# Layer 3 of a four-layer graph kernel: values and sums of weights in separate 32-column tiles, shares made before the transposes, some sums added on VectorE, and a new order of the work

## The chip, the cores and the metric

The kernel runs on one core of one Trainium2 chip. The metric is the time of one execution on the device in microseconds; the time of a kernel is the median over its runs. The engines named below are TensorE (PE in the profile), VectorE (DVE), ScalarE (ACT), GpSimd (POOL) and SyncE (SP). Each engine works through its own instructions strictly in the order in which the program lists them, and they meet at semaphores.

## What is computed

There are 16 graphs of 1024 nodes with 128 features, and a 0/1 adjacency matrix for each. Four layers follow each other, and each adds its result to its input and normalises the sum over the features (`x = layernorm(x + layer(x, adj))`). Layers 0 and 1 are graph attention (1 head of 128 features; 8 heads of 16), layer 2 is an average over neighbours with learned matrices. Layer 3, which the change is about, is dot-product attention with 4 heads of 32 features over the neighbours:

```python
Wh = jnp.einsum('bsf,hfd->bhsd', features, W)                    # 4 heads, D = 32
scores = jnp.einsum('bhsd,bhtd->bhst', Wh, Wh) / jnp.sqrt(jnp.float32(D))
scores = jnp.where(adj_matrix[:, None, :, :] > 0, scores, NEG_INF)
attn = jax.nn.softmax(scores, axis=-1)
h = jnp.einsum('bhst,bhtd->bhsd', attn, Wh)
```

The softmax is never made as such. The kernel makes the weights exp(score), sums weight times value and weight alone over the neighbours on TensorE, and divides the first sum by the second at the end.

## The kernel before

**Who decides the order.** The kernel does not write its instructions in the order in which they run. Each piece of work is a `step` with an engine, a planned duration, a due time (`due`) and the buffers that it reads and writes. `Plan.run` replays these steps against planned clocks: of all steps whose inputs are ready, it takes for each engine the one that can start first, and among those that could start within 0.05 us of each other the one with the earliest due time. A step is not considered before its due time is within `AHEAD` of the earliest open one. The order that comes out is written into the program and is fixed; on the chip every engine keeps to it, whatever the real durations are. Due times are offsets in a graph's own time, which advances by `PERIOD` from graph to graph, so that layer 3 of one graph is mixed with layers 0, 1 and 2 of the next ones. Planned durations are numbers in the source (`step("DVE", 1.07, at, share, ...)`).

**Buffers.** Steps claim places in pools. In PSUM there are two places `wk` of two banks each, used for scores, products and transposes, two places `acc1` of one bank (sums of layers 0 and 1) and two places `acc3` of one bank (sums of layer 3). In SBUF the pool `z` (9 places) holds the weights of layers 0 and 1, and `z3` (4 places) those of layer 3.

**Layer 1** is the largest load of VectorE: for each of 8 blocks of 128 nodes and each of 8 heads, `scalar_tensor_tensor` over 128x1024 makes the weights `z` (line 774). TensorE multiplies them with the values (line 782), with four heads side by side in 32 columns each.

**Layer 3** is the nested loop in `layer3`: two halves of 512 columns, and in each half 8 blocks `j` of 128 nodes. For a block, ScalarE makes `gap` (line 1060, very large where there is no edge), TensorE makes four heads of scores in two `wk` places (lines 1070 and 1080, in row tiles), ScalarE takes their exponential into two `z3` places of two heads each (line 1113), and `weighted` multiplies them with the values (line 1092). The values of a head carry a column of ones, so a head has 33 columns and takes a 64-column tile; one call of `weighted` covers two heads, and a block needs two calls. The two accumulators `av` hold values and sum of weights together.

At the end of a half ScalarE copies both accumulators to `oT` (line 1129), TensorE transposes 8 blocks (line 362), and VectorE takes the reciprocals of the sums, one per node and head (`share`, lines 1140 and 1143), multiplies, and adds the result to `x3` (line 1154).

**Around it.** `before3` prepares layer 3: a transposed input, the product with the weights in a `wk` place, a copy `whT`, seven small copies that turn the heads by groups of 32 rows (`turn`, lines 1004 and 1006, read from the same `wk` place), a transpose of those, the values `hh3`, and a bound on the scores from squared norms (lines 1030 and 1037). Each layer ends in `layernorm`: VectorE makes `off` (line 420), ScalarE squares eight blocks (line 426), VectorE makes the variance (line 437), GpSimd takes its power -1/2 (line 442), VectorE makes `shift` (line 448), ScalarE applies both (line 454). Layer 2's goes on with gamma, beta, relu and a sum on VectorE (lines 951, 958, 965) and a second normalisation.

Of the kernel before, what the change touches and what calls it, by code (L numbers as in the profile page):

```python
# [20 lines left out]
F32 = mybir.dt.float32  # L21
BF16 = mybir.dt.bfloat16
I32 = mybir.dt.int32
AF = mybir.ActivationFunctionType
# [52 lines left out]
class Plan:  # L77
# [6 lines left out]
    SLACK = 0.00  # L84
    SWITCH = 0.1
    SAME = 0.0
    AHEAD = 327.0

    def __init__(self):
        self.steps = []  # L90
        self.places = {}
        self.users = {}
        self.turns = {}

# [8 lines left out]
    def step(self, engine, us, due, emit, reads=(), writes=(), lag=None, holds=(), floor=0.0, mode="full"):  # L103
# [28 lines left out]
        follows.discard(s)  # L132
        s.waits = len(follows)
# [87 lines left out]
def tile_binary(  # L221
# [32 lines left out]
    W3 = D3 + 1  # L254
    F8 = mybir.dt.float8e5
    PAD1 = 32 - W1
    PAD3 = 64 - W3
# [10 lines left out]
    make_identity(nc, ident)  # L268
    far = const.tile([P, P], BF16, name="far")
# [17 lines left out]
    LATER1 = 3.4  # L287
    LATER3 = 13.7
# [27 lines left out]

    plan.pool("wk", wks)
# [5 lines left out]
    places("z3", 4, [P, 2, HALF])  # L323
    places("oT1", 1, [P, N])
    places("oT3", 1, [P, N])
# [17 lines left out]
    for t in places("hh3", 3, [P, HB, H3 * W3 + PAD3]):  # L343
        nc.vector.memset(t[:, :, : H3 * W3].rearrange("p k (h c) -> p k h c", c=W3)[:, :, :, D3:], 1.0)
        nc.vector.memset(t[:, :, H3 * W3 :], 0.0)
# [629 lines left out]
    def before3(b, due):  # L975
# [7 lines left out]
        def heads(hh):  # L983
            return hh.t[:, :, : H3 * W3].rearrange("p k (h c) -> p k h c", c=W3)[:, :, :, :D3]

        for chunk in range(2):
# [5 lines left out]
                [xT, w3c], [(ps, 0)], holds=[hh, whT, turn],  # L992
# [3 lines left out]
                [(ps, 0)], [whT],  # L996
            )

            def turned_groups(turn=turn, ps=ps):
                for h in range(H3):  # L1000
                    rows_h = slice(h * D3, (h + 1) * D3)
                    into = blocks_of(turn.t[rows_h, :])
                    of = blocks_of(ps.t[rows_h, :HALF])
                    nc.scalar.copy(into[:, :, h * D3 :], of[:, :, : P - h * D3])  # L1004
                    if h:
                        nc.scalar.copy(into[:, :, : h * D3], of[:, :, P - h * D3 :])

            step("ACT", 2.6, due + chunk, turned_groups, [(ps, 0)], [turn])
            step(
                "PE", 0.44, due + chunk,  # L1010
                lambda turn=turn, ps=ps: transposes(
                    ps.t[:, HALF:], [turn.t[:, k * P : (k + 1) * P] for k in range(HB)]
                ),
                [turn], [(ps, 1)],
# [3 lines left out]
                lambda hh=hh, ps=ps: nc.scalar.copy(  # L1018
                    heads(hh), ps.t[:, HALF:].rearrange("p (k h d) -> p k h d", k=HB, h=H3)
                ),  # L1020
                [(ps, 1)], [hh],
# [3 lines left out]
        sq, norms, bound = Buf("oT3", "sq"), little("norms", [P, NB * H3]), little("bound", [P, 1])  # L1025
        low = G["low"] = little("low", [P, 1])
        for n, hh in enumerate(hhs):
            step(
                "ACT", 0.48, due,
                lambda n=n, hh=hh: nc.scalar.activation(  # L1030
                    sq.t.rearrange("p (c k h d) -> p c k h d", c=2, k=HB, h=H3)[:, n], heads(hh), AF.Square
                ),
                [hh], [(sq, n)],
            )

        def largest():
            nc.vector.tensor_reduce(norms.t, sq.t.rearrange("p (n d) -> p n d", d=D3), AX.X, ALU.add)
            nc.vector.tensor_reduce(bound.t, norms.t, AX.X, ALU.max)

        step("DVE", 1.35, due, largest, [sq], [norms, bound])  # L1040
# [8 lines left out]
    def layer3(b, due, span):  # L1049
        G = graphs[b]  # L1050
        x3, m, whTs, turns, low, hhs = G["x3"], G["m"], G["whT"], G["turn"], G["low"], G["hh3"]
        tot = little("tot", [P, NB])
        for half in range(2):
            cols = slice(half * HALF, (half + 1) * HALF)
            av = [Buf("acc3", f"av3_{g}") for g in range(2)]
# [33 lines left out]
            def weighted(j, g, z, av=av):  # L1089
# [80 lines left out]

    PERIOD = 133.3
    weights(-190)
    for b in range(B):
        at = b * PERIOD
# [637 lines left out]
```

## Time and profile before

| | |
|---|---|
| median of 3 runs | 2353.89 us (2352.1 to 2354.01) |
| profiled execution | 2357.02 us, span of its instructions 2355.2 us |
| PE, PE weight loads | 2144.1 us (91%), 996.5 us (42%) |
| DVE, ACT, POOL | 1875.7 us (80%), 1707.9 us (73%), 286.7 us (12%) |
| mean granted TensorE clock | 0.976 |

Busy time is the union of an engine's instructions. A matmul in float32 stands in the trace as two instructions, and four column tiles run side by side, so the mean length of one matmul says little; the distance from the start of one group to the start of the next is what TensorE really spends. From about 459 us to 2145 us one stretch of 135.04 us repeats, one for each graph; before it the pipeline of graphs fills, and after 2145 us only layers 2 and 3 of the last graphs are left.

### The profile page before, as it was taken

How to read it: one execution, taken by the hardware profiler on the slowest of the kernel's cores; microseconds unless marked ns; L12 is line 12 of the kernel's file. 1: busy time of each engine (PE TensorE's matmuls, PEld its weight loads, DVE VectorE, ACT ScalarE, POOL GpSimd, SP SyncE). 2: the span in 40 equal slices, each digit the busy share in tenths (PEclk: the TensorE clock that was granted, in tenths of full speed). 3: DMA queues.
4: the chain of work that ended last, by engine and by line, in shares of the span. 5: the costliest groups of instructions: out<-in, count | busy, mean ns of one | idle time of the engine just before them, and what ended most of it. 6: DMA issues, size and time to landing. Idle time of an engine off the chain costs nothing.

```text
span 2355.2 us, 47149 instructions
## 1 busy us (share of the span) xinstructions
PE 2144.1 (91%) x19376; PEld 996.5 (42%) x19376; DVE 1875.7 (80%) x2616; ACT 1707.9 (73%) x4214; POOL 286.7 (12%) x268
## 2 busy tenths in 40 slices
PE   5758899999999999999999999999999999998776
PEld 5515354443625445352534444363544436242321
DVE  4899888979797988979797897979789797995201
ACT  3414669698786969788686869868686987869675
POOL 2001011111011111111011111101111110110000
PEclk8879999999999999999999999999999999999988
DMA  6222221313122221312232131313213031200000
GB/s 103 57 65 32 82 37 52 72 24 87 32 82 37 83 40 24 87 41 78 33 95 31 33 92 24 84 26 97 32 57 66 14 87 24 73 10 10 1 10 11
DMA packets 80817, 119.32 MB, mean 51 GB/s; under 512 B 7384, under 2 KB 58704, under 8 KB 80592
## 3 DMA queue, kind: packets, MB, share of 16 engines
q1 hardware_dynamic: 62160, 99.43, 13.1%
q0 software_dynamic: 18432, 16.79, 8.7%
q8 instruction: 154, 2.52, 0.4%
q14 instruction: 71, 0.58, 0.1%
HBM read 157.55 MB, written 8.97 MB: 71 GB/s over the span
## 4 chain that ended last, share of the span: by engine, by line
PE 52%; DVE 24%; ACT 19%; issue 2%; POOL 1%; DMA 1%; POOLq 0%; DVEq 0%; ACTq 0%
PE acc L1092 15%; DVE z L774 13%; PE acc L782 10%; PE wk L1080 7%; PE acc L634 7%; ACT z L1113 5%; ACT junk L426 4%; PE wk L371 4%; PE wk L362 3%; ACT x L454 3%; PE wk L1070 2%; ACT turn L1004 2%; PE wk L914 2%; DVE tot L401 2%; DVE x L935 1%
## 5 line engine op out<-in xcount | busy, mean ns | idle before, releaser
L774 DVE SCALAR_TENSOR_TENSOR z<-R,q,m 128x1024 f32<-128x1024 f32 x1024 | 1249.8, 1278 | 53.2 <-PE acc L782 45.4
L1092 PE MATMUL acc<-z,hh 128*64 128x512 f32 x2048 | 546.9, 621 | 70.8 <-ACT z L1113 70.8
L1113 ACT ACTIVATE z<-wk,low 128x1024 f32<-128x1024 f32 x512 | 542.6, 1105 | 74.4 <-PE wk L1080 74.4
L782 PE MATMUL acc<-z,hh 128*32 128x512 f32 x4096 | 517.3, 615 | 60.6 <-DVE z L774 58.0
L426 ACT ACTIVATE junk<-x,off 128x128 f32<-128x128 f32 x640 | 257.3, 402 | 302.6 <-DVE off L420 286.0
L442 POOL TENSOR_TENSOR rstd<-rstd,b_neg_half 128x8 f32<-128x8 f32 (+1 forms) x81 | 176.1, 2174 | 1308.1 <-DVE rstd L437 1192.2
L1080 PE MATMUL wk<-whT,turn 32*128 32x512 f32 x2048 | 295.8, 647 | 0.0
L454 ACT ACTIVATE x<-x,shift,rstd 128x128 f32<-128x128 f32 x640 | 256.5, 488 | 31.7 <-DVE shift L448 31.7
L1092 PEld LDWEIGHTS acc<-z,hh 128*64 128x64 f32 x2048 | 106.4, 136 | 393.8 <-ACT z L1113 196.0
L634 PEld LDWEIGHTS acc<-hd,z 128*128 128x128 f32 x2048 | 243.6, 195 | 67.0 <-issue 18.5
L782 PEld LDWEIGHTS acc<-z,hh 128*32 128x32 f32 x4096 | 103.6, 110 | 389.5 <-issue 205.9
L634 PE MATMUL acc<-hd,z 128*128 128x129 f32 x2048 | 259.9, 282 | 7.0 <-DVE z L622 3.8
L914 PEld LDWEIGHTS <-m 128*128 128x128 fp8e5 x3072 | 178.6, 98 | 16.9 <-issue 16.8
L914 PE MATMUL wk<-y,m 128*128 128x128 bf16 (+1 forms) x3072 | 181.7, 220 | 3.6 <-DVE y L900 1.3
L1060 ACT ACTIVATE gap<-m,neg_one 128x512 bf16<-128x512 fp8e5 x256 | 183.6, 720 | 0.0
L622 DVE SCALAR_TENSOR_TENSOR z<-R,q,m 128x512 f32<-128x512 f32 x240 | 164.8, 745 | 4.6 <-DMA R<-rows 4.6
L1070 PEld LDWEIGHTS <-far 32*32 32x32 bf16 x4096 | 36.1, 88 | 209.1 <-issue 207.2
L1070 PE MATMUL wk<-gap,far 32*32 32x512 bf16 x4096 | 115.4, 388 | 6.8 <-ACT z L1113 2.9
L426 ACT ACTIVATION_READ_ACCUMULATOR junk<-x,off 128x1 f32 x640 | 120.6, 188 | 0.0
L1080 PEld LDWEIGHTS wk<-whT,turn 32*128 32x128 f32 x2048 | 80.8, 185 | 59.2 <-issue 59.2
L543 POOL DMA_DIRECT2D m<-in_adj_dram x128 | 73.0, 577 | 222.1 <-ACT gap L1060 205.9
L951 DVE TENSOR_TENSOR x<-x,b_gamma_bc 128x1024 f32<-128x1024 f32 x16 | 19.6, 1225 | 91.2 <-ACT x L454 91.2
(114 smaller groups left out, 1729.9 us busy)
## 6 DMA issues: line engine op xcount, KB each, us to landing
R<-rows SPq DMA_DIRECT2D x139, 512.0 KB
m<-in_adj_dram POOLq DMA_DIRECT2D x128, 128.0 KB, 4.4
xT<-in_xT_dram SPq DMA_DIRECT2D x32, 256.0 KB
x<-in_x_dram SPq DMA_DIRECT2D x16, 512.0 KB
out_dram<-x SPq DMA_DIRECT2D x15, 512.0 KB
rows<-rT SPq DMA_DIRECT2D x16, 32.0 KB
out_dram<-x SPq DMA_DIRECT2D x2, 256.0 KB
z<-in_L_gnn_a_dram SPq DMA_DIRECT2D x2, 128.0 KB
```

The costliest lines, as they stand in the source:

```text
L426: nc.scalar.activation(junk.t, y.t[:, k, :], AF.Square, bias=off.t[:, k : k + 1], accum_out=squared.t[:, k : k + 1])
L442: lambda: nc.gpsimd.tensor_tensor(rstd.t[:, ks], rstd.t[:, ks], neg_half[:, ks], ALU.pow),
L454: nc.scalar.activation(y.t[:, k, :], y.t[:, k, :], AF.Identity, bias=shift.t[:, k : k + 1], scale=rstd.t[:, k : k + 1])
L634: nc.tensor.matmul(av[k // 2].t.rearrange("p (k c) -> p k c", k=2)[:, k % 2, : P + 1], lhsT=z.t[:, at : at + P], rhs=hd.t[:, j, : P + 1], ...
L774: nc.vector.scalar_tensor_tensor(z.t, in0=G["R"][h].t, scalar=q.t[:, j, h : h + 1], in1=m[j].t, op0=ALU.max, op1=ALU.mult)
L782: nc.tensor.matmul(av[half].t[32 * c : 32 * c + 32, :], lhsT=hh.t[:, j, at : at + 32], rhs=zs[c].t[:, half * HALF : (half + 1) * HALF], st ...
L914: nc.tensor.matmul(ps.t[:, k * SLOT : k * SLOT + part.stop - part.start], lhsT=m[j].t[:, rows_i], rhs=y2.t[:, j, part], start=j == 0 and n ...
L1060: nc.scalar.activation(gap.t, m[j].t[:, cols], AF.Square, bias=neg_one, accum_out=squares[:, at : at + 1], saturate=False)
L1070: nc.tensor.matmul(sc[h // 2].t[c * 32 : (c + 1) * 32, (h % 2) * HALF : (h % 2 + 1) * HALF], lhsT=far[rows_r, rows_r], rhs=gap.t[rows_r, : ...
L1080: nc.tensor.matmul(sc[h // 2].t[:, (h % 2) * HALF : (h % 2 + 1) * HALF], lhsT=turns[j // HB].t[rows_h, j % HB * P : (j % HB + 1) * P], rhs ...
L1092: nc.tensor.matmul(av[g].t[64 * h : 64 * h + 64, :], lhsT=hhs[j // HB].t[:, j % HB, at : at + 64], rhs=z.t[:, h, :], start=j == 0, stop=j ...
L1113: lambda g=g, sc=sc, zs=zs: nc.scalar.activation(zs[g].t.rearrange("p h n -> p (h n)"), sc[g].t, AF.Exp, bias=low.t, scale=S3),
```

## The change

In `layer3` one call of `weighted` now covers all four heads, in tiles of 32 columns, without the columns of ones. A second call, `summed`, multiplies the same weights with a constant 128x32 block of ones, so that the sums of weights come out in an accumulator of their own, repeated over the 32 rows of each head. For block 3 of each half VectorE first adds the weights of block 2 to those of block 3 (two instructions of 128x1024), and one `summed` call then serves both blocks. At the end of a half VectorE takes the reciprocal of the whole accumulator of sums (128x512), multiplies the accumulator of values with it, and TensorE transposes 4 blocks instead of 8; the sum with `x3` then reads PSUM. ScalarE's two copies are gone.

In `before3` the turned copies read `whT` in SBUF rather than the `wk` place, their transposes take a `wk` place of their own, and the norms are reduced in two instructions instead of one. `z3` has 5 places instead of 4. In the plan, ScalarE and VectorE steps that hold a place in `wk`, `acc1` or `acc3` are due 67.5 us earlier than their number says, and several due times, `AHEAD` and `PERIOD` have other values.

```diff
+    URGENT = 67.5
-    AHEAD = 327.0
+    AHEAD = 346.0
...
+        if engine in ("ACT", "DVE") and any(buf.pool in self.scarce for buf in s.bufs):
+            s.due -= self.URGENT
...
+    ones = const.tile([P, D3], F32, name="ones")
+    nc.vector.memset(ones, 1.0)
...
+    TOGETHER = {(0, 3), (1, 3)}
-    LATER1 = 3.4
-    LATER3 = 13.7
+    LATER1 = 7.4
+    LATER3 = 15.9
...
+    plan.scarce = ("wk", "acc1", "acc3")
-    places("z3", 4, [P, 2, HALF])
+    places("z3", 5, [P, 2, HALF])
...
-            av = [Buf("acc3", f"av3_{g}") for g in range(2)]
+            values, sums3 = Buf("acc3", "values"), Buf("acc3", "sums")
...
+            def weighted(j, zs, values=values):
+                for h in range(H3):
+                    rows_h = slice(h * D3, (h + 1) * D3)
                     nc.tensor.matmul(
+                        values.t[rows_h, :],
+                        lhsT=hhs[j // HB].t[:, j % HB, rows_h],
+                        rhs=zs[h // 2].t[:, h % 2, :],
...
+            def summed(j, zs, sums3=sums3):
+                for h in range(H3):
+                    nc.tensor.matmul(
+                        sums3.t[h * D3 : (h + 1) * D3, :],
+                        lhsT=ones,
+                        rhs=zs[h // 2].t[:, h % 2, :],
...
-                for g in (0, 1):
+                step(
+                    "PE", 0.87, at + LATER3, lambda j=j, zs=zs, f=weighted: f(j, zs), [*zs, hhs[j // HB]], [values],
+                    mode="32 columns",
+                )
+                if (half, j) in TOGETHER:
+                    for g in (0, 1):
+                        step(
+                            "DVE", 1.2, at,
+                            lambda g=g, zs=zs, before=before: nc.vector.tensor_tensor(
+                                zs[g].t, zs[g].t, before[g].t, ALU.add
+                            ),
+                            [before[g]], [zs[g]],
+                        )
+                if (half, j + 1) in TOGETHER:
+                    before = zs
+                else:
                     step(
+                        "PE", 0.87, at + LATER3, lambda j=j, zs=zs, f=summed: f(j, zs), zs, [sums3], mode="32 columns"
                     )
...
+            step("DVE", 0.6, at, lambda sums3=sums3, rest=rest: nc.vector.reciprocal(flat(rest), sums3.t), [sums3], [rest])
+            step(
+                "DVE", 0.6, at,
+                lambda values=values, rest=rest, oT=oT: nc.vector.tensor_tensor(oT.t, values.t, flat(rest), ALU.mult),
+                [values, rest], [oT],
+            )
+            step(
+                "PE", 0.44, at,
+                lambda oT=oT, pt=pt: transposes(pt.t, [oT.t[:, k * P : (k + 1) * P] for k in range(HB)]),
                 [oT], [pt],
             )
...
-    PERIOD = 133.3
-    weights(-190)
+    PERIOD = 131.4
+    weights(-213)
     for b in range(B):
         at = b * PERIOD
-        at0 = 32 if b == 1 else at
-        before0(b, at0 - 51)
+        at0 = 71 if b == 1 else at
+        before0(b, at0 - 52)
         layer0(b, at0)
-        before1(b, at - 77)
-        layer1(b, at + 83, 128)
-        last1(b, at + 212)
-        layer2(b, at + 223)
-        before3(b, at + 199)
-        layer3(b, at + 301, 141)
+        before1(b, at - 70)
+        layer1(b, at + 82, 123)
+        last1(b, at + 184)
+        layer2(b, at + 147)
+        before3(b, at + 175)
+        layer3(b, at + 302, 133)
```

In the changed kernel the matmuls with the values stand at line 1098, those with ones at line 1108, the added weights at line 1143, the reciprocal at line 1156, the multiplication at line 1159, the sum with `x3` at line 1170 and the reduced norms at line 1033.

## Prediction

> **What bounds the kernel now.** I read the page's first two parts, then the windows, then VectorE's waits in one repeating stretch, then TensorE's timeline and the groups by form.
>
> ```profile
> PE 2144.1 (91%) x19376; PEld 996.5 (42%) x19376; DVE 1875.7 (80%) x2616; ACT 1707.9 (73%) x4214; POOL 286.7 (12%) x268
> ...
> PE   5758899999999999999999999999999999998776
> ...
> DVE  4899888979797988979797897979789797995201
> ```
>
> The whole-run shares hide three regimes: filling, an even middle at 9, and a tail (last four slices) in which VectorE has almost nothing. The windows (columns: window, length, busy time and instructions of each engine, clock) give one stretch of the middle, and the tail:
>
> ```profile
> 593.80:728.80 135.00, 130.35 (x1209) 60.60 (x1207) 116.89 (x163) 106.12 (x263) 18.05 (x16) 1.00 0.24 56
> ...
> 2145.00:2355.00 210.00, 153.09 (x1288) 53.92 (x1284) 34.60 (x92) 143.73 (x298) 11.53 (x9) 0.90 0.03 9
> ```
>
> Per graph TensorE is busy 130.4 of 135.0 us and waits 4.6: it is the bound. VectorE is second: 116.9 busy, 18.1 idle. Its waits in the same stretch (who for whom: total, times, longest):
>
> ```profile
> DVE x L951 <- ACT x L454: 6.6, 1, 6.6
> DVE z L774 <- PE acc L782: 3.5, 2, 2.1
> DVE shift L448 <- POOL rstd L442: 2.2, 2, 1.8
> DVE rstd L437 <- ACT junk L426: 2.1, 1, 2.1
> DVE norms L1037 <- ACT oT L1030: 1.2, 1, 1.2
> ```
>
> 10.5 us of that (6.6, 1.8 and 2.1) is one place: layer 2's first normalisation, where nothing stands between VectorE's own steps.
>
> **TensorE: what is saved.** Prices come from the starts of successive groups:
>
> ```profile
> 510.60 2.78 PE L782 MATMUL acc<-z,hh 128*32 128x512 f32 x24 [0.20 <-ACT x L655]
> ...
> 520.98 1.07 PE L782 MATMUL acc<-z,hh 128*32 128x512 f32 x8
> 521.98 1.08 PE L1092 MATMUL acc<-z,hh 128*64 128x512 f32 x4
> ...
> 528.96 0.66 PE L362 MATMUL wk<-b_ident,x 128*128 128x128 f32 x4
> 529.54 2.23 PE L371 MATMUL wk<-w1c,xTc 128*128 128x144 f32 x16
> ...
> 557.37 1.09 PE L362 MATMUL wk<-b_ident,oT 128*128 128x128 f32 x8
> 558.39 1.92 PE L782 MATMUL acc<-z,hh 128*32 128x512 f32 x16
> ```
>
> Three column steps take 2.78, one 1.07: (2.78 - 1.07)/2 = 0.855 us each. Alone, a step of 32 columns starts 1.00 before a step of 64, so each change of tiling costs 0.145 more. A 64-column call (4 instructions, two heads) takes as long as a 32-column call with all four heads. Per half there were 16 calls; now 8 with values and 7 with ones. One less in each half: 2 x 0.855 = 1.7 us per graph. In the order of both programs, unbroken runs of one column tiling fall from 699 (425 of 64 columns, 274 of 32) to 442, since values, ones and layer 1 now share a tiling: 257 x 0.145 / 16 = 2.3. Transposes: 8 take 1.02, 4 take 0.58: 2 x 0.44 = 0.9. Sum 4.9 us, leaving TensorE 125.5 busy per graph. If VectorE allowed it, that would be 12.5 stretches x 4.9 = 61 us.
>
> **VectorE: what is added.**
>
> ```profile
> L951 DVE TENSOR_TENSOR x<-x,b_gamma_bc 128x1024 f32<-128x1024 f32 x16 | 19.6, 1225 | 91.2 <-ACT x L454 91.2
> L831 DVE TENSOR_TENSOR x<-wk,rd 128x512 f32<-128x512 f32 x32 | 22.1, 692 | 1.1
> L827 DVE RECIPROCAL rd<-wk 128x32 f32<-128x32 f32 x32 | 11.3, 353 | 2.0 <-PE wk L362 1.1
> L1143 DVE TENSOR_TENSOR rest<-wk,rd 128x256 f32<-128x256 f32 x64 | 24.2, 420 | 1.1
> L1140 DVE RECIPROCAL rd<-wk 128x16 f32<-128x16 f32 x32 | 8.1, 252 | 35.4 <-PE wk L362 35.4
> L932 DVE RECIPROCAL rd<-degrees 128x4 f32<-128x4 f32 x32 | 5.7, 178 | 1.1
> ```
>
> The reciprocal is the point of this case. From 4 to 16 elements its time grows by (252 - 178)/12 = 6.2 ns an element, from 16 to 32 by (353 - 252)/16 = 6.3. An ordinary operation grows by (1225 - 692)/512 = 1.04. So 128x512 costs 153 + 512 x 6.25 ns = 3.35 us, where the plan allows 0.6. The bounds are 0.69 (if it ran like line 831's operation of the same shape) and 3.35; I take 3.35, because three reciprocals lie on one line and that line is the operation itself.
>
> The Trainium skill ("VectorE: DVE Perf Modes", section "The DVE is not a fixed-function vector unit" and its walkthrough of the hardware budget) says that Reciprocal is an iterative division with a repeat count of 8, where other operations give a result a cycle. That speaks against this change; the trace has six times the ordinary slope, not eight. By eight times 1.04 ns it would be an estimated 4.4 us, and the final sum some 26 us higher.
>
> Per graph, VectorE gets: reciprocals 2 x 3.35 = 6.7; multiplications 2 x 0.69 = 1.4; added weights 4 x 1.225 = 4.9; norms in two reductions (2 x 0.68 as line 401's, for 1.22) 0.15. It loses 2 x (0.25 + 2 x 0.42), in the timeline 2 x 1.0 = 2.0. The sum with `x3` stays 0.69. Net +11.1: VectorE is busy 128.0 us per graph, more than TensorE. The bound changes engines.
>
> **What idle time VectorE keeps.** In the new order nine instructions of layer 0 (0.68 each) stand inside layer 2's normalisation. Following ScalarE's order there with its rows (eight squares 4.3 us; then exponentials, two copies and one gap 4.1; eight applications 3.2), I find 0.8 + 0.2 + 0.9 = 1.9 us of waits instead of 10.5. Against that, the path from layer 2's last `shift` to the norms gets longer on ScalarE: before it took 13.9 us (631.06 to 644.92); now two exponentials (2.1) and two applications of layer 0 (0.7) stand ahead of the last square, so 16.6. VectorE has some 12 us of work there, and the `z` places are full meanwhile: 3.8 to 4.7 us idle, where it was 1.2. Both waits start and end on VectorE, so being late does not absorb them. Waits for `z` places, 3.5, I halve to 1.6, since TensorE now has 5 us more room (bounds 0 and 3.5). Gaps without a name stay 1.2. Sum 1.9 + 3.8 + 1.2 + 1.6 = 8.5 (bounds 4.5 and 11). The stretch becomes 128.0 + 8.5 = 136.5 us against 135.04: +1.5, and over 12.5 stretches (459 to 2145 us) **+18 us**.
>
> **Filling and tail.** Before 459 us lie one and a half layers 3, 16.6 us more VectorE work; VectorE idles 28 us between 200 and 459. I take +5 (bounds 0 and 17). In the tail the last chain gets longer: two calls instead of one after the last exponential (+0.86), then reciprocal and multiplication (4.04) and 4 transposes (0.58) for copy (0.58), 8 transposes (1.0), `share` (1.0): +2.9. At two other ends of halves TensorE's transposes stand right behind the last sums and wait 4 us for VectorE, where a block of scores filled that time: +6. The added weights make the next sums wait 2.45 us, up to four times: +5. Against it: one block less after layer 1's end (31 to 30, 3.8 each) and about 0.25 us less on each of 30 blocks: -11. Sum **+3** (bounds -8 and +14).
>
> **Edits that I cost at nothing.** ScalarE loses four copies of 0.58 us; it is busy 106 of 135. Turned copies from SBUF keep number and shape, and the earlier release of `wk` shows, if anywhere, in TensorE's 3.5 us of waits for exponentials, which TensorE's new slack covers. Transfers move with their due times on the SP and POOL queues; they fill 24% in the stretch and nobody waits for them. The reciprocal waits for the last sums, and behind it stand the multiplication and layer 1's `z`; the added weights wait for the values' matmuls, and TensorE's sums wait for them, with transposes and the next values queued behind: 4.5 us at one block, 3.5 at the other. They vanish in TensorE's slack (136.5 - 125.5), and cost that much if it is gone. The urgent due times change the order only, which is counted above.
>
> Sum: 18 + 5 + 3 = 26 on the profiled 2357.0, so 2383; the median lies 3.1 lower: **2380**.
>
> **Rivals.** (1) *Faster, 0.27.* The slots that I read as waits are covered, because an engine that is late finds its inputs ready; the 8.5 shrinks to 4.5 and the stretch to 132.5: 12.5 x -2.5 = -32, tail -4: 2318. For it: TensorE has 4.9 us to give, and most of the 18.1 us was waiting. It decides wherever VectorE's idle time falls below 7.0 a graph. With a reciprocal at the lower bound the stretch is 131.2, and the time 2307. (2) *Much slower, 0.15.* TensorE's waits add up in its fixed order: 4.5 + 3.5 for added weights, 3.5 for exponentials, 1 for `wk`: 125.5 + 12.5 = 138, and with VectorE waiting for `z` in turn 139: +50, filling +8, tail +6: 2418. Against it: the two engines rarely stand at once. (3) *No difference, 0.08*: saved and added cancel, 2354. The forecast itself has 0.50, with a range of its own of 2358 to 2410.
>
> A measurement of this kernel can tell about 0.2%, 4.7 us, from no change. The range of 2322 to 2415 leaves out the better half of rival 1 and part of rival 2.
>
> **What would show it.** Right: the reciprocal's row at about 3.3 us, VectorE at 86% with a stretch of 136 to 137 us and TensorE's waits above 10. Wrong: a reciprocal near 0.7, or a stretch below 134 with VectorE's waits under 6 us; then VectorE hides more than I allow.

## The result, and the profile after

| | before | after |
|---|---|---|
| median | 2353.95 us | 2421.59 us (2418.45 to 2422.82) |
| ratio | | 1.0287, interval 1.0269 to 1.0304 |
| profiled execution, span | 2357.02 us, 2355.2 us | 2421.31 us, 2419.5 us |
| mean granted TensorE clock | 0.976 | 0.961 |

The change costs 67.6 us; 26 were forecast. The page of the changed kernel, in the same lines as before (busy time of each engine, then tenths in 40 slices):

```profile
PE 2122.6 (88%) x21040; PEld 991.1 (41%) x21040; DVE 2037.9 (84%) x2659; ACT 1684.1 (70%) x4150; POOL 284.4 (12%) x268
...
PE   5758799899999999999999989999999989898876
...
DVE  3899789889989898999989898999999979898322
```

TensorE lost 21.5 us of work and VectorE gained 162, yet neither is at 100%. Three stretches by window, each from one graph's layer 2 to the next one's (length, then TensorE, its weight loads, VectorE, ScalarE, GpSimd, and the granted clock):

```profile
1451.45:1587.20 135.75, 126.96 (x1311) 60.20 (x1311) 125.53 (x165) 104.36 (x260) 16.94 (x16) 1.00 0.24 56
1174.89:1313.79 138.90, 128.30 (x1310) 60.20 (x1310) 127.11 (x166) 104.49 (x260) 17.59 (x16) 0.99 0.23 55
757.42:897.63 140.21, 130.21 (x1310) 60.52 (x1310) 128.40 (x167) 104.71 (x260) 18.32 (x16) 0.98 0.23 54
```

TensorE and VectorE are now both busy 125 to 130 us of a graph, and both keep some ten idle. At full clock this stretch takes 135.75 us; where the clock is 0.98 it takes 140.2, and TensorE is busy 130.2 instead of 127.0 us with the same work. Of the ten stretches between graphs 2 and 12 only two stay at full clock (136.36 and 135.75 us). VectorE's largest waits in the second:

```profile
DVE norms L1033 <- ACT oT L1028: 3.5, 2, 2.5
DVE shift L452 <- POOL rstd L446: 2.0, 2, 1.6
DVE degrees L935 <- PE wk L918: 1.9, 2, 1.6
DVE rd L670 <- PE acc L638: 1.3, 2, 1.1
```

The 6.6 us of layer 2's normalisation is gone, as counted; over the whole run that wait falls from 91.2 to 13.0 us. The new instructions, by groups:

```profile
L1156 DVE RECIPROCAL rest<-acc 128x512 f32<-128x512 f32 x32 | 107.2, 3351 | 39.0 <-PE acc L1108 39.0
L1143 DVE TENSOR_TENSOR z<-z,z 128x1024 f32<-128x1024 f32 x64 | 76.7, 1219 | 15.0 <-PE acc L1098 14.3
L1159 DVE TENSOR_TENSOR oT<-acc,rest 128x512 f32<-128x512 f32 x32 | 22.1, 692 | 1.1
```

**Where the time went.** I take the starts of layer 2's 192 matmuls as marks, one for each graph, and cut the span in three (times in us):

| | to graph 2 | graphs 2 to 14, twelve stretches | graph 14 to the end |
|---|---|---|---|
| before | 454.9 | 1621.5 | 278.9 |
| after | 479.9 | 1673.4 | 266.2 |
| difference | +25.1 | +51.9 | -12.7 |
| forecast | +5 | +18 (12.5 stretches) | +3 |

Ten of the twelve stretches go from 135.28 to 138.36 us, +30.8 together; the last two, before graph 14, hold the other 21.1. A reciprocal that stands in every half alike does not explain so uneven a loss, so I looked at the two ends for something else. The trace shows where VectorE stands. GpSimd's timeline (start, length, instruction, in brackets the idle time ahead of it):

```profile
425.85 2.65 POOL L446 TENSOR_TENSOR rstd<-rstd,b_neg_half 128x8 f32<-128x8 f32 x1 [9.27 <-DVE rstd L441]
438.51 0.38 POOL L398 PARTITION_ALL_REDUCE all<-top  x1 [10.01 <-issue]
...
1954.98 0.39 POOL L398 PARTITION_ALL_REDUCE all<-top  x1 [7.83 <-DVE top L579]
1965.77 1.68 POOL L446 TENSOR_TENSOR rstd<-rstd,b_neg_half 128x8 f32<-128x8 f32 x1 [10.39 <-issue]
```

VectorE's timeline at the same places, and the windows around the first of them:

```profile
438.92 0.23 DVE L586 TENSOR_SCALAR r<-hd,all 128x8 f32<-128x8 f32 x1 [8.95 <-POOL all L398]
...
1967.48 0.17 DVE L452 TENSOR_TENSOR shift<-off,rstd 128x8 f32<-128x8 f32 x1 [11.71 <-POOL rstd L446]
```

```profile
400.00:425.00 25.00, 22.07 (x213) 8.22 (x213) 24.51 (x26) 17.06 (x47) 2.98 (x2) 1.00 0.04 12
425.00:450.00 25.00, 15.78 (x149) 4.18 (x145) 14.40 (x21) 16.96 (x38) 3.64 (x3) 0.80 0.58 175
```

"issue" means that the profile shows nothing that GpSimd waits for. It appears when GpSimd turns from a power (line 446) to an all-reduce (line 398) or back, and lasts 6.8 to 10.4 us in this run; where the second is needed later than that, nothing is seen. VectorE stands 9 and 12 us for it, TensorE runs dry, and the granted clock of the 25 us around each of the two is 0.80. Per graph the old order has the all-reduces in two groups among the powers, the new one in three: six turns instead of four. GpSimd's waits of this kind (total, times, longest), before and after:

```profile
POOL rstd L442 <- issue: 15.4, 2, 8.4
```

```profile
POOL rstd L446 <- issue: 85.4, 11, 10.4
POOL all L398 <- issue: 10.0, 1, 10.0
```

Two of them, ahead of the first power of the program and behind its last all-reduce, stand in both kernels; the new order adds ten. The rows undercount, because a view of waits names whatever ended last. In the kernel before, GpSimd's delay is put down to weights that the power does not read:

```profile
POOL rstd L442 <- DVE z L774: 100.5, 14, 8.1
```

These are turns from an all-reduce to a power, one in most graphs, and VectorE hardly waits behind them: 0.4 us in the stretch that the prediction shows.

### The profile page after: what moved, and what is told of

It is laid out like the page before. It is cut to its first block, busy times and chain, and to the rows that moved or that the text cites. A ratio compares the mean times of both kernels' runs of the same rounds, so it can differ in the third digit from the quotient of the medians.

```text
span 2419.5 us, 50524 instructions
## 1 busy us (share of the span) xinstructions
PE 2122.6 (88%) x21040; PEld 991.1 (41%) x21040; DVE 2037.9 (84%) x2659; ACT 1684.1 (70%) x4150; POOL 284.4 (12%) x268
## 4 chain that ended last, share of the span: by engine, by line
DVE 39%; PE 36%; ACT 17%; issue 5%; DMA 2%; POOL 2%; POOLq 0%; DVEq 0%; ACTq 0%
DVE z L778 24%; PE wk L918 7%; PE acc L786 6%; PE acc L638 6%; ACT z L1129 5%; PE wk L1086 4%; PE acc L1098 4%; DVE rest L1156 4%; PE wk L366 3%; ACT junk L430 3%; PE acc L1108 3%; ACT turn L1003 2%; ACT x L458 2%; DVE z L1143 2%; PE wk L1076 2%
## 5 line engine op out<-in xcount | busy, mean ns | idle before, releaser
L786 PE MATMUL acc<-z,hh 128*32 128x512 f32 x4096 | 526.0, 628 | 80.0 <-DVE z L778 75.0
L458 ACT ACTIVATE x<-x,shift,rstd 128x128 f32<-128x128 f32 x640 | 261.6, 490 | 46.3 <-DVE shift L452 46.2
L1098 PE MATMUL acc<-z,hh 128*32 128x512 f32 x2048 | 280.0, 616 | 14.1 <-DVE rest L1156 14.1
L1108 PE MATMUL acc<-z,ones 128*32 128x512 f32 x1792 | 261.1, 614 | 28.7 <-DVE z L1143 27.8
L786 PEld LDWEIGHTS acc<-z,hh 128*32 128x32 f32 x4096 | 115.1, 113 | 390.7 <-issue 209.1
L638 PE MATMUL acc<-hd,z 128*128 128x129 f32 x2048 | 252.9, 280 | 10.4 <-ACT x L659 8.9
L1076 PE MATMUL wk<-gap,far 32*32 32x512 bf16 x4096 | 133.9, 389 | 50.4 <-ACT z L1129 19.1
L1076 PEld LDWEIGHTS <-far 32*32 32x32 bf16 x4096 | 43.0, 88 | 265.2 <-issue 262.9
L1156 DVE RECIPROCAL rest<-acc 128x512 f32<-128x512 f32 x32 | 107.2, 3351 | 39.0 <-PE acc L1108 39.0
L1108 PEld LDWEIGHTS acc<-z,ones 128*32 128x32 f32 x1792 | 50.1, 110 | 184.5 <-issue 120.2
L1098 PEld LDWEIGHTS acc<-z,hh 128*32 128x32 f32 x2048 | 48.8, 110 | 150.0 <-issue 123.6
## 6 DMA issues: line engine op xcount, KB each, us to landing
m<-in_adj_dram POOLq DMA_DIRECT2D x128, 128.0 KB, 4.7
z<-in_L_gnn_a_dram SPq DMA_DIRECT2D x2, 128.0 KB
```

The costliest lines, as they stand in the source:

```text
L458: nc.scalar.activation(y.t[:, k, :], y.t[:, k, :], AF.Identity, bias=shift.t[:, k : k + 1], scale=rstd.t[:, k : k + 1])
L638: nc.tensor.matmul(av[k // 2].t.rearrange("p (k c) -> p k c", k=2)[:, k % 2, : P + 1], lhsT=z.t[:, at : at + P], rhs=hd.t[:, j, : P + 1], ...
L786: nc.tensor.matmul(av[half].t[32 * c : 32 * c + 32, :], lhsT=hh.t[:, j, at : at + 32], rhs=zs[c].t[:, half * HALF : (half + 1) * HALF], st ...
L1076: nc.tensor.matmul(sc[h // 2].t[c * 32 : (c + 1) * 32, (h % 2) * HALF : (h % 2 + 1) * HALF], lhsT=far[rows_r, rows_r], rhs=gap.t[rows_r, : ...
L1098: nc.tensor.matmul(values.t[rows_h, :], lhsT=hhs[j // HB].t[:, j % HB, rows_h], rhs=zs[h // 2].t[:, h % 2, :], start=j == 0, stop=j == NB - 1,
L1108: nc.tensor.matmul(sums3.t[h * D3 : (h + 1) * D3, :], lhsT=ones, rhs=zs[h // 2].t[:, h % 2, :], start=j == 0, stop=j == NB - 1,)
```

## The experiments

Ratios are to the kernel before on the same chip (medians of 2353.9 to 2362.1 us there), so I compare ratios: 0.001 is 2.35 us. Most edits change only what a step emits; the plan sees the same steps, and the order on every engine stays.

**1. The reciprocal's work.** The theory was that VectorE's work through the reciprocal is the main cause.

```diff
-nc.vector.reciprocal(flat(rest), sums3.t)
+nc.vector.tensor_scalar(flat(rest), sums3.t, 1.0, None, ALU.mult)
```

> The changed kernel with the reciprocal of 128x512 replaced by a multiplication by one of the same shape, in the same place and with the same planned duration, so the order of every engine stays; layer 3's division is left out. If VectorE's load is what costs (theory 1), each of the 32 loses 3.35 - 0.69 = 2.66 us, 5.3 us a graph, and some 12 to 14 graphs run at VectorE's pace: 2421 - 64 to - 75, that is 2346 to 2357, and the repeating stretch falls from 138 to about 133 us. If the lost time lies in the new order with its waits for GpSimd (theory 2), VectorE only waits longer and less than half of that comes back: above 2385.

Measured: 2341.3 us, ratio 0.9947 (0.9929 to 0.9966), 5 us below the first range. The row of the product, in the groups of this run:

```profile
L1156 DVE TENSOR_SCALAR rest<-acc 128x512 f32<-128x512 f32 x32 | 22.0, 688 | 43.7 <-PE acc L1108 43.7
```

85.2 us were taken off VectorE and 80 came back: the reciprocal's extra time counts nearly in full, and without it the change would be a small gain.

**2. GpSimd's turns.** The same edit in the kernels after and before:

```diff
-nc.gpsimd.partition_all_reduce(got.t, v.t, P, op)
+nc.gpsimd.tensor_copy(got.t, v.t)
```

> The changed kernel with GpSimd's all-reduce over partitions in the four layers replaced by a copy of the same operand, with the same planned duration; the maxima are then those of each partition alone. If GpSimd's change between the power and the all-reduce costs 7 to 10 us each time it is not hidden (theory 2), the gaps of 7 to 10 us before its instructions go, and with them VectorE's waits of 5.3 us at 265, 9.0 at 439, 11.7 at 1967 and 3.2 at 2103 us: 20 to 40 us less, 2380 to 2400. If only VectorE's load counts (theory 1), under 8 us less: above 2413.

> The kernel before with the same edit as the run without all-reduces. Its order has two groups of all-reduces for each graph where the changed kernel's has three, and VectorE waits for GpSimd 1.8 us in a stretch. Theory 2: the change of work is hidden there, so at most 8 us less (2346 to 2354). If it fell by 20 us or more, the change of work would cost both kernels alike and would explain nothing of the difference.

Measured: 2382.9 us, ratio 1.0124 (1.0087 to 1.0161), after; 2344.7 us, 0.9951 (0.9933 to 0.9969), before. So GpSimd's turns cost the new order 38 us and the old one 11, a little more than the 8 us that were allowed there. The copy takes about as long as the all-reduce (0.61 against 0.71 us in the mean); what goes is the distance. In the changed kernel no power starts less than 6.8 us after an all-reduce and no all-reduce less than 8.3 us after a power; with the copy the shortest distances are under 0.2 us, and the row with `z L774` is gone. VectorE's waits for GpSimd, first the changed kernel's, then with the copy:

```profile
DVE shift L452 <- POOL rstd L446: 55.3, 33, 11.7
DVE r L586 <- POOL all L398: 10.0, 3, 9.0
```

```profile
DVE shift L452 <- POOL rstd L446: 22.8, 18, 6.7
DVE r L586 <- POOL all L398: 0.7, 2, 0.4
```

They fall by 41.8 us together, about what the time fell by. The first of them in the kernel before, without and with the copy:

```profile
DVE shift L448 <- POOL rstd L442: 51.3, 34, 4.8
```

```profile
DVE shift L448 <- POOL rstd L442: 40.5, 20, 4.8
```

The wait for the power is nearly as long there (51.3 against 55.3 us), but only 10.8 us of it come from the turns.

With GpSimd's turns out of both kernels, the filling differs by 14.2 us instead of 25.1 (465.8 against 451.6), and the twelve stretches by 33.9 instead of 51.9.

**3. Both at once.** The two diffs above in one kernel.

> The changed kernel with its order untouched, with both edits that were run alone: the reciprocal becomes a product with 1.0 of the same shape (the division is left out) and GpSimd's all-reduce becomes a copy (maxima of each partition alone). Alone they gave -80 and -38 us. If VectorE's load and GpSimd's change of work are two separate causes, the sum holds: 2421.6 - 80 - 38 = 2303, 2293-2312 us, below the kernel before by some 50 us. If a lighter VectorE takes in GpSimd's delays (or they are two sides of one wait), less than half of the 38 us is left: 2325-2342 us.

Measured: 2302.5 us, ratio 0.9754 (0.9730 to 0.9778). Alone the edits took off 0.0340 and 0.0163, together 0.0533: within the intervals they are separate and add up. That gives an account of the whole change, with the reciprocal counted as what it takes beyond a product of the same shape: everything but reciprocal and turns, 0.9754 against 0.9951, is -46 us; the reciprocals on top, 1.0124 against 0.9754, +87 us; the turns that the new order adds, (1.0287 - 1.0124) - (1 - 0.9951), +27 us. The sum is the +68 by construction; what the runs say is the split, with some 10 us of uncertainty on each part.

**4. The same reciprocal in the kernel before**, where VectorE has 18 us of each stretch free. If work counts only once VectorE is full, most of this should hide.

```diff
 def share(pt=pt, rd=rd, o=o):
     pn = ...
+    nc.vector.reciprocal(o.t.rearrange("p k c -> p (k c)"), pt.t[:, :HALF])
```

> The kernel before with its order untouched; each of its 32 steps that make shares does one more reciprocal of 128x512 (3.35 us by the row of the changed kernel), whose output is written over at once. Theory load (VectorE bounds a stretch only once its busy time comes near the stretch): VectorE's busy time rises from 116.9 to 123.6 us of a stretch of 135.0, still 11 us under it, so much of the 107 us is hidden: the time rises by 10 to 45 us, to 2364-2399 us. Theory place (what stands at the end of a half of layer 3 lies on the loop that sets the stretch, however busy VectorE is): the time rises by 75 to 107 us, to 2429-2461 us.

Measured: 2462.4 us, ratio 1.0455 (1.0407 to 1.0504): +106.7 us, which is 32 x 3.33. None of it is seen to be hidden. A stretch by window:

```profile
603.61:745.32 141.71, 133.06 (x1211) 60.85 (x1207) 123.25 (x165) 106.11 (x263) 17.64 (x16) 0.99 0.23 53
```

VectorE still has 18.5 us free, as before (135.0 - 116.9 = 18.1): the idle time stayed and the stretch grew by 6.7. In the stretches of this run at full clock (141.37 us) it grew by 6.33, and VectorE is busy 6.34 us longer. The whole run's clock is lower than before, too (0.966 against 0.976), so its 3.33 us for each are not VectorE's time alone. Idle time in a fixed order need not be room. It stands ahead of certain instructions, and work put elsewhere only moves them back. TensorE's waits, before and in this run, show who closes the loop:

```profile
PE acc L782 <- DVE z L774: 58.0, 38, 7.4
```

```profile
PE acc L782 <- DVE z L774: 78.6, 49, 7.4
...
PE wk L1070 <- DVE rest L1143: 34.9, 15, 2.4
```

The wait for VectorE's `rest` is new. Behind the reciprocal on VectorE stand the products that free a `wk` place for the next scores, and layer 1's `z`, for which TensorE waits.

**5. The additions.** They load VectorE by 76.7 us.

```diff
-zs[g].t, zs[g].t, before[g].t, ALU.add
+zs[g].t[:, :, :2], zs[g].t[:, :, :2], before[g].t[:, :, :2], ALU.add
```

> The changed kernel with its order untouched; the 64 additions of weights on VectorE (L1143, 1219 ns each) cover only 2 of 512 columns of each head, so that most of their time is gone and some of the weights are left out of the sums. Theory 1 (VectorE's load sets the stretch of a graph, whatever instruction makes the load): some 4.6 us a graph go from VectorE, and as the cheap share gave back 5.0 us a graph for 5.3 us taken, the time falls by 60 to 75 us, to 2346-2362 us. Rival (the reciprocal hurts because it stands between the last sums and the transposes, not by its load; the additions lie beside TensorE's work): the time falls by less than 30 us, to 2392 us or more.

Measured: 2411.0 us, ratio 1.0201 (1.0174 to 1.0229), 20 us below the changed kernel, where VectorE's busy time fell by 63. My theory missed by 40 us. VectorE's waits tell why; first the changed kernel's:

```profile
DVE rstd L441 <- ACT junk L430: 30.6, 21, 8.0
...
DVE rd L831 <- PE wk L366: 6.4, 1, 6.4
...
DVE x L853 <- ACT oT L849: 1.2, 1, 1.2
```

and without the additions:

```profile
DVE rstd L441 <- ACT junk L430: 47.2, 32, 8.0
...
DVE rd L831 <- PE wk L366: 15.3, 11, 6.4
DVE x L853 <- ACT oT L849: 10.1, 14, 1.6
```

These three groups alone take 34 of the 63 us back (the trace is that of the longest of the four executions, 2418.8 us). Nearly all of the waits that are new begin at the end of an addition: behind it stands an instruction that waits for squares, transposes or exponentials, and these do not come sooner. So an instruction counts by its place: the additions lie mostly ahead of waits, the reciprocals mostly ahead of work that others wait for.

**6. Other plans.** Here the plan sees other steps, and the order changes everywhere. First the reciprocal's true length; then no additions; shares after transposing and no additions; the old due times; and the new due times with the old layer 3.

```diff
-step("DVE", 0.6, at, ... nc.vector.reciprocal(
+step("DVE", 3.35, at, ... nc.vector.reciprocal(
```

> The changed kernel with the reciprocal's planned duration set to 3.35 us instead of 0.6, so that only the order changes. Theory 1 (load): VectorE still has 127 us of work for each graph, so the time stays within 15 us, 2406 to 2436. Theory 3 (the order was made for durations that are wrong, and that is what costs): the waits go and most of the 67 us comes back, below 2385.

```diff
-TOGETHER = {(0, 3), (1, 3)}
+TOGETHER = set()
```

> The changed kernel without the weights added on VectorE (no block is joined, 16 calls with ones for each graph instead of 14). VectorE gets 4.9 us less for each graph (127 to 122), TensorE 1.7 us more. Theory 1 (VectorE's load sets the stretch): 138.4 - 4.9 = 133.5 us, so 2421 - 12.5 x 4.9 = 2360, between 2350 and 2375. Theory 2 (GpSimd's changes of work in the new order): they stay, so less than 20 us comes back, above 2400.

```diff
+TOGETHER = set()
+step("ACT", 0.48, at, ... nc.scalar.copy(sT.t, sums3.t))
+step("ACT", 0.48, at, ... nc.scalar.copy(vT.t, values.t))
+step("PE", 0.93, at, ... 8 transposes of sT and vT)
+step("DVE", 0.95, at, share, ...)    # reciprocal of 128x16, one product
```

> The 32-column tiles for values and ones stay, no weights are added on VectorE, and the shares are made after the transposes again: ScalarE copies both accumulators, TensorE transposes 8 blocks, VectorE takes reciprocals of 128x16. VectorE falls to about 116 us a graph, TensorE has 128. Theory 1: TensorE is the bound again, with its 5 us of waits the stretch is 132 to 134 us and the time 2320 to 2345, below the kernel before. Theory 2: GpSimd's changes of work in this order cost what they cost in the changed kernel, so 2350 to 2370.

```diff
 # layer 3 of after
+AHEAD = 327.0; LATER1 = 3.4; LATER3 = 13.7; PERIOD = 133.3
+plan.scarce = ()                     # and before's due times
```

> The changed layer 3 with the plan's numbers of before (due times, AHEAD, PERIOD, LATER1, LATER3, no step made urgent). Theory 1: VectorE's load is the same, and the old order has nothing inside layer 2's normalisation, where 10.5 us of waits come back: 2421 + 0 to + 60. Theory 2 or 3 (the new numbers are the fault): faster than the changed kernel by 20 us or more, under 2400.

```diff
 # layer 3 of before
+URGENT = 67.5; AHEAD = 346.0; LATER1 = 7.4; LATER3 = 15.9; PERIOD = 131.4
+plan.scarce = ("wk", "acc1", "acc3") # and after's due times
```

> The layer 3 of before with the plan's numbers of the changed kernel and its urgent steps: the order alone. Theory 1: VectorE has room (117 us a graph), TensorE is the bound, so the time stays near before, 2335 to 2375. Theory 2 (the new order's waits for GpSimd cost by themselves): 2375 to 2395. Theory 3 (the numbers fit only the new layer 3): above 2395.

Measured: 2526.3 (ratio 1.0722), 2507.9 (1.0638), 2603.3 (1.1058), 2596.3 (1.1022) and 2429.9 us (1.0324); the intervals are 0.002 to 0.003 to either side. The first, third and fourth missed what every theory gave them; the second and fifth lie above the limit that one theory set. None of the five says what its part is worth: a new order of all the work outweighs it. They have one row in common, GpSimd's waits without a releaser (here without additions):

```profile
POOL rstd L446 <- issue: 148.2, 19, 10.9
POOL all L398 <- issue: 48.2, 5, 10.7
```

It was 15.4 us in the kernel before, 95.4 in the changed one and, in the order of the five, 163, 196, 311, 166 and 108: large in all, but not in step with the time. To test it, the kernel without additions with the edit of experiment 2:

> The re-planned kernel without the additions (2507.9 us), with GpSimd's all-reduce made a copy (maxima of each partition alone), in the same order as that kernel. If GpSimd's change of work is what makes re-planned orders slow (196 us of delays ahead of its instructions there), at least half of the 86 us that it lost against the changed kernel comes back: 2380-2450 us. If the order is slow in itself: over 2470 us.

Measured: 2451.6 us, ratio 1.0403 (1.0381 to 1.0424). The turns cost this order 55 of its 150 us. That is more than the 38 us of the changed kernel, but not most of the loss. With the same edit in both, this order is still 66 us slower than the changed kernel's (1.0403 against 1.0124); why stays open.

**7. Other engines for reciprocal and power.** ScalarE makes both through a logarithm and an exponential, in the old place of the step.

```diff
-nc.vector.reciprocal(flat(rest), sums3.t)
+nc.scalar.activation(flat(rest), sums3.t, AF.Ln); nc.scalar.activation(flat(rest), flat(rest), AF.Exp, scale=-1.0)
-nc.gpsimd.tensor_tensor(rstd.t[:, ks], rstd.t[:, ks], neg_half[:, ks], ALU.pow)
+nc.scalar.activation(rstd.t[:, ks], rstd.t[:, ks], AF.Ln); nc.scalar.activation(..., AF.Exp, scale=-0.5)
```

> The changed kernel with its plan untouched: each share is made by ScalarE as the exponential of minus the logarithm (two 128x512 instructions, some 0.6 us each, at the place of VectorE's reciprocal), and each power of -0.5 by ScalarE as the exponential of -0.5 times the logarithm instead of GpSimd's power, so that GpSimd has no change of work between power and all-reduce. Theories 1 and 2 together: VectorE loses 107 us and the mean delays of GpSimd go, as in the run with both cheap edits, against some 60 us more on ScalarE, which has a third of its time free, and some table loads: 2285-2330 us, faster than the kernel before. Rival (ScalarE's queue is no free room: the logarithm waits for the last sums in front of the exponentials of the next scores, and TensorE stands): 2350-2420 us.

The power alone, in the kernel before:

> The kernel before with its plan untouched; each power of -0.5 by ScalarE (exponential of -0.5 times the logarithm) instead of GpSimd's power. Theory 2: GpSimd's changes of work cost the kernel before little, as the run with the all-reduce taken out showed (-10.7 us), but the power's 2.2 us of latency goes as well: 2325-2348 us. Rival: the power's latency and the change of work lie beside other work, and ScalarE's extra instructions and table loads push its queue back: 2350-2375 us.

Measured: 2723.5 us, ratio 1.1545 (1.1508 to 1.1581), and 2569.9 us, 1.0877 (1.0846 to 1.0908), both far above either range. The groups of the first:

```profile
L446 ACT ACT_TABLE_LOAD x162 | 207.8, 1283 | 2.9
L1156 ACT ACT_TABLE_LOAD x64 | 82.1, 1283 | 1.0
```

Each logarithm and each exponential behind it loads a table, two loads for each power, where I had allowed for some. ScalarE does this in front of work that others wait for: in the second run TensorE's wait for the exponentials of layer 3 is 171.9 us, where it was 70.8 before. The Trainium skill ("ScalarE: Activation LUTs", "Table sets: the hidden batching unit") names a set that holds both functions and would need one load for the pair; these programs did not get it. The 1283 ns that the page gives for a load (section "What ACT_TABLE_LOAD costs") are what the trace shows.

**8. The tiling without the large reciprocal**, in the order of the changed kernel. The sums of block `k` of 128 columns go to row `k` of each head's 32, so that all sums fit 128x128; they are copied, transposed beside the values, and divided afterwards.

```diff
+for k in range(HB):
     for h in range(H3):
-        nc.tensor.matmul(sums3.t[h * D3 : (h + 1) * D3, :], lhsT=ones, rhs=zs[h // 2].t[:, h % 2, :], ...)
+        nc.tensor.matmul(sums3.t[h * D3 : (h + 1) * D3, :P], lhsT=ones[:, HB - 1 - k : HB - 1 - k + D3],
+                         rhs=zs[h // 2].t[:, h % 2, k * P : (k + 1) * P], ...)   # ones: column HB - 1 is 1, the rest 0
-nc.vector.reciprocal(flat(rest), sums3.t)
+nc.scalar.copy(total, sums3.t[:, :P])     # second run: nc.vector.tensor_copy, here and below
-nc.vector.tensor_tensor(oT.t, values.t, flat(rest), ALU.mult)
+nc.scalar.copy(oT.t, values.t)
 # 4 transposes of oT, now 1 of total; then, ahead of the sum with x3:
+nc.vector.reciprocal(share, of_head)      # 128x16
+nc.vector.tensor_tensor(n, n, share.to_broadcast([P, HB * H3, D3]), ALU.mult)
```

> The changed kernel with its order untouched. Sums are made by block of 128 columns into one 128x128 region (four times as many products, each a quarter as wide), sums and values are copied by ScalarE (0.25 and 0.6 us), transposed together (5 instead of 4 transposes), and VectorE takes a reciprocal of 128x16 and multiplies after transposing. VectorE loses 3.1 us in each half (101 us in all), ScalarE gets 27 us. As the cheap share gave back 80 of 85 us, 85 to 100 us come back here: 2322-2337 us, faster than the kernel before by some 1%. Rival (ScalarE's two copies wait for the last sums in front of the next exponentials, or the narrow products are slow): 2350-2420 us.

> The same with both copies on VectorE: it loses 2.3 us in each half (74 us in all), and ScalarE is left alone. By load, 65 to 75 us come back: 2346-2357 us, slower than the kernel with ScalarE's copies by some 20 us. If ScalarE's copies were what hurts there, this one is the faster of the two.

Measured: 2384.1 us, ratio 1.0122 (1.0079 to 1.0165), and 2380.2 us, 1.0108 (1.0080 to 1.0135): the same within their intervals, 39 and 42 us below the changed kernel, half of what was expected. The narrow products are not slow (rows of the changed kernel, then of the second run):

```profile
L1108 PE MATMUL acc<-z,ones 128*32 128x512 f32 x1792 | 261.1, 614 | 28.7 <-DVE z L1143 27.8
```

```profile
L1119 PE MATMUL acc<-z,ones 128*32 128x128 f32 x7168 | 253.8, 279 | 38.9 <-DVE z L1154 38.9
```

The second run's stretch is 134.6 us, against 132.5 with the cheap share. Where the other half went is not settled. TensorE's wait for the additions has grown by 11 us in the rows above, and its wait for the `wk` place that the new end of a half reads for longer is 11.1 us, where that place made it wait 0.4 us with the cheap share:

```profile
PE wk L1086 <- DVE x L1066: 11.1, 18, 2.2
```

Both runs also let the two `junk` places of the squares share one tile; no run separates that.

**9. A plan that knows GpSimd's turns.** In the plan a power starts no earlier than 8.5 us after an all-reduce, and the other way round; steps that hold `wk`, `acc1` or `acc3` are urgent in both; `AHEAD`, `URGENT`, `PERIOD` and the due times were chosen anew by the plan's own end. Once with experiment 8's layer 3 and no additions, once with the layer 3 of before.

```diff
 # Plan.start
+if s.engine == "POOL" and s.mode in ("power", "maxima") and s.mode != self.work:
+    t = max(t, now + 8.5)
 # Plan.run
+if s.engine == "POOL" and s.mode in ("power", "maxima"):
+    self.work = s.mode
```

> New tiling with sums by block and shares after transposing, as in the run with copies on VectorE, no additions, and a plan in which a power on GpSimd starts no earlier than 8.5 us after an all-reduce and the other way round, with due times chosen anew under that rule. The plan's own end is 2291 us. Theory (an order is slow when it counts on GpSimd too early): delays ahead of GpSimd's instructions no longer hold VectorE (its waits for the power under 60 us), a stretch of 128 to 133 us, and 2280-2340 us, faster than the kernel before. Rival (orders are slow because TensorE stands in short gaps and its clock falls): over 2390 us.

> The layer 3 of the kernel before (64-column tiles, shares after transposing) with the same rule for GpSimd and due times chosen anew under it. The plan's own end is 2321 us, 30 us above the other. If the new tiling is worth what TensorE's rows say (4.9 us a graph), it is 20 to 70 us slower than the run with the new tiling: 2310-2380 us. If the tiling is worth nothing, the two are within 10 us.

Measured: 2364.2 us, ratio 1.0040 (1.0015 to 1.0065), and 2327.7 us, ratio 0.9881 (0.9852 to 0.9911). The second is faster than both kernels, by 1.2% than before and by 3.9% than after. VectorE's wait for the power there, to be set beside 51.3 before:

```profile
DVE shift L458 <- POOL rstd L452: 20.3, 20, 3.1
```

How much of it is the rule and how much are the new due times and urgent steps was not taken apart. The new tiling did not win, against my expectation, though the two orders differ in more than the tiling. Its run met the condition (VectorE waits 11.4 us for the power) and yet lies between the two ranges, with a mean stretch of 136.3 us instead of 128 to 133. It has a wait for layer 1's rows to arrive, which are read back by DMA (3.8 us before):

```profile
DVE z L789 <- DMA R<-rows: 55.4, 15, 5.1
```

## Why the prediction was wrong

**Right: the operations.** The reciprocal was priced at 3.35 us from three small ones and measures 3351 ns; the multiplication at 0.69 measures 692, an addition at 1.225 measures 1219. By the repeat count of 8 that the prediction cites from the Trainium skill ("VectorE: DVE Perf Modes", "First, the fixed hardware budget") it would have been an estimated 4.4 us; the rows have six times the ordinary slope, and the measurement decides. TensorE was to fall from 130.4 to 125.5 us of a graph: 127.0 in the stretch at full clock, 3.4 of the 4.9 us. VectorE was to reach 128.0: 125.5 to 128.4.

**Right at full clock, but not for the reason given: the stretch.** Forecast was 136.5 us; the two stretches at full clock take 135.75 and 136.36, the mean of ten is 138.4, and 136.9 with GpSimd's turns out. Over the old stretch that is 3.1 us where 1.5 were forecast. The count of waits place by place held: layer 2's 10.5 us shrank to at most 2.6 (1.9 forecast), the norms' wait is 2.7 to 3.5 us (3.8 forecast). It left out waits for layer 2's degrees (1.9 us) and layer 0's sums (up to 1.3). At full clock VectorE is busy 2.5 us less than forecast and idle 1.7 us more; that these cancel is luck. But "the bound changes engines" is not needed for a reciprocal to cost its time: experiment 4 shows it counted in full on a VectorE with 18 us free, and experiment 5 shows additions counted by a third on a VectorE with ten.

**The step that failed: "Edits that I cost at nothing."** It says that the urgent due times "change the order only, which is counted above". The count covered TensorE, VectorE and ScalarE; the order on GpSimd's queue was not followed. In the runs its turns cost 11 us in the old order and 38 in the new one, which has two more per graph: +27 us of the 41.6 that were missed, at a price of nothing in the sum. The trace of before held the evidence: the two waits "issue" of up to 8.4 us, and the 14 waits of up to 8.1 us that it puts down to `z`.

**The term that was too small: filling.** +5 was forecast with bounds of 0 and 17, and 25.1 measured. GpSimd has 11 of it; of the 14.2 that stay without its turns, the reciprocals have 6.5 (465.8 against 459.3 us), and the other 7.7 are open. My ground for a small number, VectorE's 28 us of idle time before 459 us, is the error that experiment 4 shows: idle time that I took for room. That it was none before 459 us is argued from there, not shown.

**The term with the wrong sign: the tail.** +3 was forecast, within -8 and +14, and -12.7 measured from graph 14 on. The two long stretches just before it (147.1 and 142.7 us, where 136.2 and 132.5 stood) lost more than the marks here give back, so the division between them is not sharp: together they are +8.4.

**The clock** was in no term. Before, it is at full speed from 300 to 2175 us; after, it falls to 0.93 (13 times) or 0.80 (twice) in 15 windows of 25 us between 400 and 2200 us, each time while TensorE stood idle or within 2 us after it. It had stood for 1.2 to 4.5 us where the clock is 0.93, and for 5.2 and 7.5 us where it is 0.80; after other stands of 2 us it did not fall. By these windows, an estimate of what the lower clock takes from TensorE is at most 13 x 1.75 + 2 x 5 = 33 us. No run separates its share: the waits beside it went together with it, so it can be part of each of the three numbers of experiment 3.

**Rivals.** The faster one (late engines find their inputs ready) needed reciprocals at 0.69 us to come near: 2341 us with them. The much slower one, 2418 us, gave nearly the right time, but for another reason: it put 8 us a graph on TensorE's waits for additions, and these are 27.8 us in the whole run (the row in experiment 8), 1.7 a graph. That it came near is luck.

## What to carry to other kernels

In a program of fixed order, ask of each added instruction what stands behind it on its engine: if that is work others wait for, it counts in full however idle the engine looks, and if that is a wait, it may be free. Follow every queue that a new order touches, also that of an engine busy for 12% of the time, and look between unlike instructions for waits without a releaser, or with one that the waiting instruction does not read. To learn what one part of a scheduled change costs, change what a step emits and leave the plan's numbers alone; a new plan brings an order of its own, worth more than the part.

## What was not expected of the hardware

- In the changed kernel GpSimd needs 6.8 to 10.4 us between a power and an all-reduce, in either direction, counted from the end of the first and hidden if the second is needed later. The Trainium skill ("GPSIMD Engine Reference", "2.1 Instruction dispatch") gives about 6 us for the first call of freshly loaded code, with no instruction in the profile. Runs with a copy for the all-reduce lose the delay between the two, which fits; that it is code loading, no run here shows.
- A reciprocal costs some 6.25 ns for each element of a partition: 178, 252, 353 and 3351 ns for 4, 16, 32 and 512 elements.
- Matmuls with ones, 128 columns wide in 32-column tiles, take 254 us in 7168 instructions where 512 columns took 261 in 1792.
- Of 15 stands of TensorE of 1.8 to 2.6 us in the changed kernel (400 to 2200 us), nine are followed by a clock of 0.93 in the 25 us around them.
